# Layer 2's gathered rows as 1024 bytes of mirrored features, in fixed buffers

## The chip, the cores and the metric

The kernel runs on one core of a Trainium2 chip. The core has five engines that work side by side, each through its own instructions in program order: TensorE (PE, matrix products, with PEld for its weight loads), VectorE (DVE), ScalarE (ACT), GpSimd (POOL) and SyncE (SP). Sixteen DMA engines move data. An engine waits for another through semaphores. The metric is the device time of one execution in microseconds (us); the median of several runs counts.

## The reference

The reference is a graph attention network of two layers on 6250 nodes and 100,000 edges, sorted by destination. After a layernorm and relu of x, each layer computes, for node features h = x W:

```python
alpha_s = (h * a_src[None]).sum(-1)
alpha_d = (h * a_dst[None]).sum(-1)
e = jax.nn.leaky_relu(alpha_s[src] + alpha_d[dst], NEG_SLOPE)
m = jax.ops.segment_max(e, dst, num_segments=n)
e = jnp.exp(e - m[dst])
denom = jax.ops.segment_sum(e, dst, num_segments=n)
alpha = e / (denom[dst] + 1e-16)
out = jax.ops.segment_sum(h[src] * alpha[:, :, None], dst, num_segments=n)
```

Every node has an edge to itself beside the listed ones. Layer 1 has four heads of 64 features, layer 2 one head of 256. After layer 2 come relu, a product with Wm1 (256 x 256), bias, relu, a product with Wm2 (256 x 768), bias, and x is added. All is float32.

## The kernel before, in words

**Tiles.** The nodes make 49 node tiles of 128. The edges make 784 edge tiles of 128, of which 782 hold edges; two make a pair, four a group, eight a unit. On average a node tile takes 8 pairs. The numbers of pairs are used below as places: "pair 8t+28" is the 28th pair after the first pair of node tile t.

**Stages.** Stage 0 (to about 170 us) does the layernorm and the features of layer 1 (L447) and writes them as rows to a table in DRAM; a copy of them, `kept`, stays in SBUF. Layer 1's edges take from about 170 to 1390 us, layer 2's from there to the end.

**The two powers of a score.** The exponential of a leaky relu is max(exp(s), exp(0.2 s)), for s the sum of the source's and the destination's score. So a source needs e1 = exp(s) and e2 = exp(0.2 s), and an edge's weight is, up to a factor of its destination, w = max(e1, e2 * rho), where rho comes from the destination. Layer 1's end (Node1.steps, L948 to L973) computes for each node tile the features h of layer 2 and its score on PE, copies the features to `kept` on ACT (L969), makes e1 and e2 there with two exponentials (`powers`, L208 and L209), sets a one between them (DVE) and writes rows of 256 + 3 floats (features, e1, 1, e2: 1036 bytes) to layer 2's table.

**Gathers.** POOL fetches the rows of an edge tile's 128 sources with one indirect DMA (L645, in `gather`) into one half of a pair's buffer. The buffers are 20 of the pool "gathered", each [128, 2, 268] floats, used in turn by both layers; a gather is issued 8 groups ahead of its use, so that of pair q has to wait until PE is done with pair q - 20.

**A pair of layer 2** (`pair`): DVE makes v = e2 * rho (L712) and w = max(v, e1) (L715) for both edge tiles, then for each tile a matrix hw (L719) that holds w at the destination's column and zero elsewhere. PE multiplies it with the gathered rows into o_ps (L736), 258 columns: 256 features, e1, which nothing reads, and the one, which gives the sum of the weights. A product in float32 stands in the trace as two records, so a pair has four. A unit, four pairs, has one PSUM buffer.

**Sums and the node steps.** After each unit DVE adds its product to what is carried over (`take_sum`, acc, L753) and ACT copies quarters of 32 rows to the node's sum (L762). When a node's sum is whole, Node2.steps runs in six pieces, at the pairs that `STEPS_AT` (L62) lists: for node tile t at 8t + 20, 21, 24, 27, 30 and 33.

1. all_ adds the node's own edge (DVE, L1054) and rden is the reciprocal of the weights' sum (L1066).
2. o = all_ * rden (ACT, L1069), turned by PE (L915).
3. rT, relu and bias (ACT, L921), and the product with Wm1 (PE, L1078).
4. mT, relu and bias (ACT, L1083), the bias of y (PE, L1027) and the first half of the product with Wm2 (PE, L1088).
5. x is added to this half (DVE, L1092), and PE makes the other half.
6. x is added to that, and the result goes out (L1117).

Once per node tile PE also makes the destinations' terms of the next 16 edge tiles from two masks (`meet`, L691); SP brings two masks of 256 KB, x's 384 KB, and takes the result away.

**Order.** The schedule is manual: each engine runs its instructions in the order in which the program issues them. So pair 8t+28 on DVE stands behind the acc at 8t+27 and ahead of all_ of the next node tile, and on ACT mT and two sum copies stand at 8t+27.

**Layer 1's early rows.** Some pairs of layer 1 (`SOON`) are gathered early from a table that is not whole yet; 23 such buffers are put away to DRAM (`soon_away`) and fetched back (`soon_back`), and what they lack is added by PE and DVE (`soon_missing`, `soon_whole`). Layer 2's first tiles are treated likewise (`first_rows`, L389). A function `general` computes everything anew for graphs that don't fit; it is not executed here.

Of the kernel before, what the change touches and what calls it, by code (L numbers as in the profile page):

```python
# [70 lines left out]
def kernel(  # L71
# [12 lines left out]
    W2T: bass.AP,  # L84
    A2: bass.AP,
    b2: bass.AP,
    Wm1: bass.AP,
# [64 lines left out]

    RW = {1: 4 * (HID // 4 + 1), 2: HID + 2}
    TW = {1: RW[1] + 8, 2: RW[2] + 1}
    table, sd = {}, {}
# [55 lines left out]
    def heads_row(row):  # L211
        return row[:, :RW[1]].rearrange("p (h c) -> p h c", h=4)

    def edge_places(ones):

        dst_i = ones.tile([P, NET], I32, name="dst_i")
        dri = ones.tile([NCH, CH], I32, name="dri")
        nc.sync.dma_start(src_i, src_cols)
        yield
        yield  # L220
        soonest = sorted(range(len(SOON)), key=SOON.__getitem__)
        for i in range(0, len(SOON), 2):
            for k in soonest[i:i + 2]:
                soon_places(k)
            yield
        for to, of in ((dst_i, dst_cols), (dri, dst_rows)):
            nc.sync.dma_start(to, of)
            yield
            yield
        for layer in bT:  # L230
            with nc.allow_non_contiguous_dma(reason="256 numbers"):
                nc.sync.dma_start(bT[layer], {1: b1, 2: b2}[layer].rearrange("(k p) -> p k", p=P))
            yield
        b = ones.tile([P, OUT_DIM // P], F32, name="b")
# [12 lines left out]
        nc.sync.dma_start(dmod_d, drm)  # L247
        bp = ones.tile([P, 3, OUT_DIM // P], BF16, name="bp")
# [46 lines left out]
    def first_whole(pool, layer):  # L295

        j = 0
        for stage, (n, there) in enumerate(EARLY[layer]):
            for k in range(n):
                pair, t = divmod(FIRST + j, 2)  # L300
                G = first_G[layer][pair][:, t]
# [17 lines left out]
    def rows_in(layer):  # L319

        return gp.tile([P, 2, max(TW.values())], F32, name="G")[:, :, :TW[layer]]

    def first_rows(layer, stage):
# [3 lines left out]
        for j in range(j, j + n):  # L327
            k, t = divmod(FIRST + j, 2)
            if k not in first_G[layer]:
                first_G[layer][k] = rows_in(layer)  # L330
            nc.gpsimd.indirect_dma_start(
                out=first_G[layer][k][:, t], out_offset=None, in_=table[layer][:there * P],
                in_offset=bass.IndirectOffsetOnAxis(ap=first_i[layer][:, j:j + 1], axis=0))
# [3 lines left out]
    soon_d = dram.tile([len(SOON), P, 2 * TW[1]], F32, name="soon_d")  # L337
    soon_G, soon_of, soon_p, soon_hit = {}, {}, {}, {}
# [18 lines left out]
    def soon_away(held):  # L357

        for i in list(soon_G)[:max(len(soon_G) - held, 0)]:
            nc.sync.dma_start(soon_d[i], soon_G.pop(i).rearrange("p t c -> p (t c)"))  # L360

    def soon_back(i):
        G = rows_in(1)
        nc.sync.dma_start(G.rearrange("p t c -> p (t c)"), soon_d[i])
        return G

# [252 lines left out]
    def layer_edges(layer, H, node, pre, matched, pre_pool):  # L619
# [4 lines left out]
        with tc.tile_pool(name=f"eg{layer}", bufs=5) as eg, \  # L624
# [9 lines left out]
            def gather(g):  # L634
                if not 0 <= g < NG:
                    return
                for t in tiles(g):
# [5 lines left out]
                    if soon or k < FIRST + len(THERE.get(layer, ())):  # L643
                        continue
                    nc.gpsimd.indirect_dma_start(  # L645
                        out=G[k // 2][:, k % 2], out_offset=None, in_=table[layer],
                        in_offset=bass.IndirectOffsetOnAxis(ap=src_i[:, k:k + 1], axis=0))
# [277 lines left out]
    with tc.tile_pool(name="w2p", bufs=1) as wp, tc.tile_pool(name="wk2", bufs=2) as wk:  # L925
# [4 lines left out]
        class Node1:  # L930
# [17 lines left out]
            def steps(self, t, sum_, most=None, last=None):  # L948
# [18 lines left out]
                yield from rest(4)  # L967
                row = kept[t][:, :TW[2]]
                nc.scalar.activation(row[:, :HID], h_ps[:, :HID], AF.Copy)  # L969
                powers(row[:, HID:HID + 1], row[:, HID + 2:], h_ps[:, HID:HID + 1])  # L970
                nc.vector.memset(row[:, HID + 1:HID + 2], 1.0)
                nc.sync.dma_start(table[2][t * P:(t + 1) * P], row)
                nc.scalar.activation(sd[2][:, t], h_ps[:, HID:], AF.Copy)  # L973

        with tc.tile_pool(name="pre1", bufs=1) as pre:
            pre1 = prepare(pre, 1, 4)
            layer_edges(1, 4, Node1(), pre1,
                        lambda: scores_in(ps, w2, *w2_in, KH, 1), pre)


    with tc.tile_pool(name="wmp", bufs=1) as wp, tc.tile_pool(name="x3", bufs=4) as xp, \
# [48 lines left out]
        class Node2:  # L1030
# [27 lines left out]
            def steps(self, t, sum_, most=None, last=None):  # L1058
# [6 lines left out]
                rden = wk.tile([P, 1], F32, name="rden")  # L1065
                nc.vector.reciprocal(rden, all_[:, HID + 1:])  # L1066
                yield 1
# [62 lines left out]
def general(ctx, tc, v):  # L1130
# [6 lines left out]
    NTP = NT + 1  # L1137
    RWG = 4 * (HID // 4 + 1)
    with ExitStack() as own:
        def pool(name, bufs, **kw):  # L1140
# [5 lines left out]
        ps = pool("gps", 2, space=bass.MemoryType.PSUM)  # L1146
        gdram = pool("gdram", 1, space=bass.MemoryType.DRAM)
        pidx = keepp.tile([P, 2], F32, name="gpidx")
        nc.gpsimd.iota(pidx, pattern=[[P, 2]], base=0, channel_multiplier=1,
# [52 lines left out]
        def chunk(layer, H, c, b):  # L1202
# [6 lines left out]
            nc.vector.tensor_copy(df, di)  # L1209
            TWl = v["TW"][layer]  # L1210
            G = wk.tile([P, TPC, TWl], F32, name="G", tag="G")
# [133 lines left out]
        for i in range(NT):  # L1345
            rT = turned(1, 4, i)
            h_ps = ps.tile([P, HID + 2], F32, name="h_ps", tag="mm")
            for k in range(KH):
                nc.tensor.matmul(h_ps, rT[:, k], w2[:, k], start=(k == 0), stop=(k == KH - 1))
            row = wk.tile([P, v["TW"][2]], F32, name="row2")  # L1350
            nc.scalar.activation(row[:, :HID + 1], h_ps[:, :HID + 1], AF.Copy)
# [84 lines left out]
```

## Time and profile before

| | |
|---|---|
| median of 3 runs | 2554.95 us (2551.26 to 2574.33) |
| profiled execution, its own time | 2563.6 us |
| its span, first to last instruction | 2561.7 us |
| mean granted TensorE clock | 0.792 of full speed |
| busy: PE / DVE / ACT / POOL | 1797.7 / 1389.5 / 411.6 / 1523.5 us |
| gathers (L645) | 1507 records, 950 ns each |
| layer 2's o_ps (L736, 258 columns) | 1564 records, 460 ns each |
| hw of layer 2 (L719) | 782, 406 ns each |

Busy time counts an engine's instructions without their waits, so an engine that is 60% busy may still be the one that is always late. A group's line gives how often an instruction ran, its busy time and mean, and then the idle time of its engine just before it with what ended that idle time. The stages have to be read apart, since each has its own limit; the trace can be asked for any stretch of the span. A few records of matrix products and gathers can be missing from it.

### The profile page before, as it was taken

To read this page: it belongs to the slowest core of one execution; us is meant where nothing else is said; L and a number is where in the kernel's file an instruction comes from. 1 tells how busy PE (TensorE), PEld (TensorE's weight loads), DVE (VectorE), ACT (ScalarE), POOL (GpSimd) and SP (SyncE) were. 2 spreads that over 40 slices of the span, in tenths; PEclk is the share of its full clock that TensorE was granted. 3 is DMA by queue.
4 is the path that set the end of the run, shared out by engine and by line. 5 is a ranking of instruction groups with operands and counts; after the bars stand their busy time and mean duration, and the time that the engine had idled before them with its cause. 6 is when DMAs were issued, how large, how long until landed. Compare 5 with 4: busy or idle time off the path is not lost.

```text
span 2561.7 us, 26528 instructions
## 1 busy us (share of the span) xinstructions
PE 1797.7 (70%) x7728; PEld 1286.3 (50%) x7729; DVE 1389.5 (54%) x4195; ACT 411.6 (16%) x1273; POOL 1523.5 (59%) x1666
## 2 busy tenths in 40 slices
PE   9952768678667668686767456777667767776677
PEld 7841546556445446455554244544444444544455
DVE  7742667567656567666656444444444434444444
ACT  6730011011111111111111011111111111111112
POOL 5257465566655565656553666666666666666661
PEclk9975788878778778877889677777877777877888
DMA  9986355455545555555543445554545455545552
GB/s 340 355 266 199 114 154 148 125 150 154 140 138 136 146 141 151 154 148 157 133 122 122 129 122 153 156 150 135 153 140 168 133 152 157 153 133 152 149 149 75
DMA packets 167328, 400.36 MB, mean 156 GB/s; under 512 B 36632, under 2 KB 54255, under 8 KB 167175
## 3 DMA queue, kind: packets, MB, share of 16 engines
q0 software_dynamic: 75072, 211.10, 30.7%
q1 hardware_dynamic: 90732, 185.99, 21.5%
q10 hardware_dynamic: 1370, 1.48, 0.2%
q8 instruction: 65, 1.06, 0.2%
q14 instruction: 89, 0.72, 0.1%
HBM read 333.87 MB, written 64.56 MB: 156 GB/s over the span
## 4 chain that ended last, share of the span: by engine, by line
PE 38%; issue 22%; DVE 18%; another core or an unknown queue 11%; POOL 6%; DMA 4%; ACT 1%; DVEq 0%; SPq 0%; POOLq 0%; ACTq 0%
PE o_ps L736 19%; PE missing L389 6%; PE y_ps L1088 5%; POOL G L645 4%; DMA G<-table,src_i 4%; PE h_ps L447 4%; DVE hot L673 3%; DVE hw L724 3%; DVE soon_hit L379 2%; DVE e_ps L722 2%; DVE e_ps L712 2%; DVE hw L719 2%; PE tp L1078 1%; DVE acc L753 1%
## 5 line engine op out<-in xcount | busy, mean ns | idle before, releaser
L645 POOL DMA_INDIRECT G<-table,src_i x1507 | 1431.4, 950 | 861.5 <-issue 381.4
L736 PE MATMUL o_ps<-G,hw 128*128 128x258 f32 x1564 | 518.0, 460 | 247.7 <-issue 183.2
L736 PE MATMUL o_ps<-hw,hot 128*128 128x260 f32 x1564 | 489.9, 448 | 232.8 <-issue 157.3
L736 PEld LDWEIGHTS o_ps<-G,hw 128*128 128x128 f32 x1564 | 349.8, 230 | 385.5 <-issue 271.6
L736 PEld LDWEIGHTS o_ps<-hw,hot 128*128 128x128 f32 x1564 | 326.9, 218 | 361.5 <-issue 217.1
L762 ACT ACTIVATE sum<-acc 32x260 f32<-32x260 f32 (+1 forms) x384 | 160.0, 417 | 1224.7 <-DVE acc L753 697.7
L389 PE MATMUL missing<-kept,soon_hit 128*128 128x268 f32 x1028 | 277.0, 422 | 61.3 <-issue 60.6
L719 DVE TENSOR_SCALAR hw<-iota_ps,dcol,w 128x128 f32<-128x128 f32 x782 | 284.9, 406 | 16.9 <-DVE w L715 2.3
L724 DVE TENSOR_TENSOR hw<-G,e_ps 128x520 f32<-128x520 f32 x391 | 271.9, 695 | 27.7 <-DVE e_ps L722 11.8
L389 PEld LDWEIGHTS missing<-kept,soon_hit 128*128 128x128 f32 x1028 | 210.9, 208 | 119.4 <-issue 80.4
L1092 DVE TENSOR_TENSOR y<-y_ps,xt 128x384 f32<-128x384 f32 (+1 forms) x98 | 54.5, 556 | 256.5 <-PE o_ps L736 70.6
L1088 PE MATMUL y_ps<-wm,mT 128*128 128x384 f32 x392 | 180.2, 589 | 18.4 <-issue 9.5
L447 PE MATMUL h_ps<-w,r 128*128 128x264 f32 (+1 forms) x588 | 142.8, 398 | 17.8 <-issue 15.3
L673 DVE TENSOR_TENSOR hot<-iota_ps,dcol 128x512 f32<-128x512 f32 x196 | 133.6, 682 | 33.5 <-remote 24.5
L396 DVE SCALAR_TENSOR_TENSOR G<-G,soon_ok,missing 128x268 f32<-128x268 f32 x46 | 22.6, 492 | 212.7 <-remote 127.9
L447 PEld LDWEIGHTS h_ps<-w,r 128*128 128x128 f32 x588 | 111.8, 197 | 41.4 <-issue 17.6
L712 DVE TENSOR_TENSOR e_ps<-G,e_ps 128x8 f32<-128x8 f32 (+1 forms) x782 | 125.2, 160 | 7.3 <-DVE hw L724 2.8
L1088 PEld LDWEIGHTS y_ps<-wm,mT 128*128 128x128 f32 x392 | 78.2, 222 | 89.6 <-issue 50.2
L691 PE MATMUL e_ps<-win,mask 128*128 128x12 bf16 (+1 forms) x1564 | 67.8, 167 | 72.4 <-issue 69.1
L1083 ACT ACTIVATE mT<-tp,bm1c 128x128 f32<-128x128 f32 x98 | 30.6, 363 | 531.6 <-PE o_ps L736 260.8
L699 DVE TENSOR_REDUCE e_ps<-e_ps 128x64 f32<-128x192 f32 (+2 forms) x98 | 27.7, 283 | 136.4 <-remote 124.5
L691 PEld LDWEIGHTS <-mask 128*128 128x128 bf16 x1564 | 60.6, 98 | 79.7 <-issue 68.6
(415 smaller groups left out, 1347.4 us busy)
## 6 DMA issues: line engine op xcount, KB each, us to landing
xt<-in_x SPq DMA_DIRECT2D x96, 384.0 KB
drow<-dmod_d SPq DMA_DIRECT2D x49, 512.0 KB
mask_d<-mask SPq DMA_DIRECT2D x97, 256.0 KB
mask<-mask_d SPq DMA_DIRECT2D x97, 256.0 KB
G<-table,src_i POOLq DMA_INDIRECT x1507
xTt<-in_xT SPq DMA_DIRECT2D x49, 384.0 KB
out<-y SPq DMA_DIRECT2D x48, 384.0 KB
table<-kept SPq DMA_DIRECT2D x49, 134.0 KB
```

What stands on the lines that cost most here:

```text
L389: nc.tensor.matmul(soon_p[k], hit[:, T - there], kept[T], start=(T == there), stop=(T == NT - 1))
L447: nc.tensor.matmul(h_ps[:, :n], r[:, k], w1[:, k, :n], start=(k == 0), stop=(k == KI - 1))
L645: nc.gpsimd.indirect_dma_start(out=G[k // 2][:, k % 2], out_offset=None, in_=table[layer], in_offset=bass.IndirectOffsetOnAxis(ap=src_i[:, ...
L673: nc.vector.tensor_tensor(hot[g][:, T[0]:T[0] + n], iota_ps.unsqueeze(1).to_broadcast([P, n, P]), dcol[:, k:k + n].unsqueeze(2).to_broadca ...
L691: nc.tensor.matmul(e_ps[t][:, at + k, :3 * H], m[:, k * P:(k + 1) * P], pre.win[:, 2 * u + 2], start=True, stop=True)
L712: nc.vector.tensor_mul(v, e2, rho)
L719: nc.vector.tensor_scalar(hw[:, t], iota_ps, dcol[:, k:k + 1], w[:, t], ALU.is_equal, ALU.mult)
L724: nc.vector.tensor_mul(hw, Gp[:, :, :RW[1]].rearrange("p t (h c) -> p t h c", h=H), w.unsqueeze(3).to_broadcast([P, 2, H, C + 1]))
L736: nc.tensor.matmul(o_ps[u], l, r[:, :RW[layer]], start=(g % 2 == 0 and k == 0), stop=(g % 2 == 1 and k == tiles(g)[-1]))
L762: nc.scalar.activation(done[t][r], acc[r], AF.Copy)
L1088: nc.tensor.matmul(y_ps, mT[:, j], wm2[:, j, s * half:(s + 1) * half], start=False, stop=(j == KH - 1))
L1092: nc.vector.tensor_add(y[:n, s], y_ps[:n], xt[:n, s * half:(s + 1) * half])
```

## The change

Layer 2's rows lose everything but 256 floats, 1024 bytes. W2's columns are multiplied by a mirror (a Householder reflection) that maps the vector a_src of layer 2 on the first axis; feature 0 of a mirrored row is then the source's score divided by the length of a_src, up to its sign. The mirror is undone on each node tile's sum, before o. In parts:

- `mirror_in` computes in stage 0 the mirror's vector, the same scaled by -2 over its squared length (`mirror_b`), and two factors per partition (`slopes`) with which feature 0 becomes s and 0.2 s. It is some 22 instructions on DVE and two on ACT, and one broadcast DMA for a_src.
- `mirrored(wk, of, to)` reflects 128 rows: a product with mirror_b, a sum over 256, and a scaled addition, three DVE instructions. It is run on the two halves of W2 at the start of layer 1, and on all_ in step 1 of each of the 49 node tiles in layer 2, after rden and ahead of o.
- In each of the 391 pairs of layer 2, ACT makes e1 and e2 of both edge tiles from feature 0 of the gathered rows, with two exponentials of [128, 2] that take their scale from `slopes`; v and w on DVE read these.
- The one that gives the weights' sum is no longer gathered: the 20 buffers are now fixed, [128, 2, 288] floats, taken in turn by a list; layer 2's rows begin at float 16 of each half, and float 272 is set to one by 20 memsets on POOL at the start. o_ps has 257 columns.
- Node1.steps no longer makes the powers (98 instructions of ACT); its store writes rows of 256 floats.
- The set-aside rows of layer 1 go to DRAM and back as [128, 2, 268] views of the wider buffers. `general` gets a table of its own.

```diff
-    RW = {1: 4 * (HID // 4 + 1), 2: HID + 2}
-    TW = {1: RW[1] + 8, 2: RW[2] + 1}
+    RW = {1: 4 * (HID // 4 + 1), 2: HID + 1}
+    TW = {1: RW[1] + 8, 2: HID}
...
+    def mirror_in(ones, a):
...
+        nc.vector.tensor_mul(sq, a, a)
+        nc.vector.tensor_reduce(n2, sq, AX.X, ALU.add)
+        nc.vector.tensor_scalar(n2, n2, 1e-30, None, ALU.add)
+        yield
+        nc.scalar.activation(t, n2, AF.Ln)
+        nc.scalar.activation(r, t, AF.Exp, scale=-0.5)
+        yield
+        for _ in range(2):
...
+        nc.vector.tensor_scalar(mirror, a, r, None, ALU.mult)
+        nc.vector.tensor_scalar(sign, a[:, 0:1], 0.0, 2.0, ALU.is_ge, ALU.mult)
+        nc.vector.tensor_scalar(sign, sign, -1.0, None, ALU.add)
+        nc.vector.tensor_add(mirror[:, 0:1], mirror[:, 0:1], sign)
+        yield
+        nc.vector.tensor_mul(sq, mirror, mirror)
+        nc.vector.tensor_reduce(t, sq, AX.X, ALU.add)
+        nc.vector.reciprocal(scale, t)
+        nc.vector.tensor_scalar(mirror_b, mirror, scale, -2.0, ALU.mult, ALU.mult)
+        yield
+        nc.vector.tensor_mul(t, n2, r)
+        nc.vector.tensor_mul(t, t, sign)
+        for k, by in enumerate((-1.0, -SLOPE)):
+            nc.vector.tensor_scalar(slopes[:, k], t, by, None, ALU.mult)
+        yield
+
+    def mirrored(wk, of, to):
+
+        x = wk.tile([P, HID], F32, name="mirror_x")
+        nc.vector.tensor_mul(x, of, mirror_b)
+        along = wk.tile([P, 1], F32, name="along")
+        nc.vector.tensor_reduce(along, x, AX.X, ALU.add)
+        nc.vector.scalar_tensor_tensor(to, mirror, along, of, ALU.mult, ALU.add)
...
-    gp = edges_stack.enter_context(tc.tile_pool(name="gathered", bufs=2 * (AHEAD + 2)))
+    gp = edges_stack.enter_context(tc.tile_pool(name="gathered", bufs=1))
+    AT = {1: 0, 2: 16}
+    buffers = [gp.tile([P, 2, 288], F32, name=f"G{i}") for i in range(2 * (AHEAD + 2))]
+    for G in buffers:
+        nc.gpsimd.memset(G[:, :, AT[2] + HID:AT[2] + RW[2]], 1.0)
...
-        return gp.tile([P, 2, max(TW.values())], F32, name="G")[:, :, :TW[layer]]
+        buffers.append(buffers.pop(0))
+        return buffers[-1][:, :, AT[layer]:AT[layer] + max(TW[layer], RW[layer])]
...
-            nc.sync.dma_start(soon_d[i], soon_G.pop(i).rearrange("p t c -> p (t c)"))
+            nc.sync.dma_start(soon_d[i], soon_G.pop(i))
...
-                        out=G[k // 2][:, k % 2], out_offset=None, in_=table[layer],
+                        out=G[k // 2][:, k % 2, :TW[layer]], out_offset=None, in_=table[layer],
...
-                e1, e2 = ((Gp[:, :, RW[1]:RW[1] + 4], Gp[:, :, RW[1] + 4:]) if layer == 1 else
-                          (Gp[:, :, HID:HID + 1], Gp[:, :, HID + 2:]))
+                if layer == 1:
+                    e1, e2 = Gp[:, :, RW[1]:RW[1] + 4], Gp[:, :, RW[1] + 4:]
+                else:
+                    e = sm.tile([P, 2, 2, 1], F32, name="e")
+                    for k in range(2):
+                        nc.scalar.activation(e[:, k], Gp[:, :, 0:1], AF.Exp, scale=slopes[:, k])
+                    e1, e2 = e[:, 0], e[:, 1]
...
-                row = kept[t][:, :TW[2]]
-                nc.scalar.activation(row[:, :HID], h_ps[:, :HID], AF.Copy)
-                powers(row[:, HID:HID + 1], row[:, HID + 2:], h_ps[:, HID:HID + 1])
-                nc.vector.memset(row[:, HID + 1:HID + 2], 1.0)
+                row = kept[t][:, :HID]
+                nc.scalar.activation(row, h_ps[:, :HID], AF.Copy)
+                nc.vector.memset(kept[t][:, HID:RW[2]], 1.0)
...
+            def weights2():
+                scores_in(ps, w2, *w2_in, KH, 1)
+                for k in range(KH):
+                    mirrored(wk, w2[:, k, :HID], w2[:, k, :HID])
...
-                nc.vector.reciprocal(rden, all_[:, HID + 1:])
+                nc.vector.reciprocal(rden, all_[:, HID:])
+                mirrored(wk, all_[:, :HID], all_[:, :HID])
                 yield 1
```

More of the change, by code (lines that the diff above doesn't have):

```diff
@@ L85 @@
     A2: bass.AP,
+    a2: bass.AP,
     b2: bass.AP,
@@ L212, in heads_row, with col @@
         return row[:, :RW[1]].rearrange("p (h c) -> p h c", h=4)
+    def mirror_in(ones, a):
+        def col(name):
+            return ones.tile([P, 1], F32, name=name)
+        n2, r, t, sign, scale = (col(f"mirror_{k}") for k in ("n2", "r", "t", "sign", "scale"))
+        sq = ones.tile([P, HID], F32, name="mirror_sq")
+        nc.vector.tensor_mul(sq, a, a)
[6 more added lines that the diff above has]
+        for _ in range(2):
+            nc.vector.tensor_mul(t, r, r)
+            nc.vector.tensor_mul(t, t, n2)
+            nc.vector.tensor_scalar(t, t, -0.5, 1.5, ALU.mult, ALU.add)
+            nc.vector.tensor_mul(r, r, t)
+            yield
[13 more added lines that the diff above has]
+            nc.vector.tensor_scalar(slopes[:, k], t, by, None, ALU.mult)
+        yield
+    def mirrored(wk, of, to):
[4 more added lines that the diff above has]
+        nc.vector.scalar_tensor_tensor(to, mirror, along, of, ALU.mult, ALU.add)
     def edge_places(ones):
@@ L233, in edge_places @@
             yield
+        a2b = ones.tile([P, HID], F32, name="a2b")
+        nc.sync.dma_start(a2b, bcast(a2, HID))
+        yield
         b = ones.tile([P, OUT_DIM // P], F32, name="b")
@@ L247, in edge_places @@
         nc.sync.dma_start(dmod_d, drm)
+        yield
+        yield from mirror_in(ones, a2b)
         bp = ones.tile([P, 3, OUT_DIM // P], BF16, name="bp")
@@ L257 @@
     bT = {layer: const.tile([P, KH], F32, name=f"bT{layer}") for layer in (1, 2)}
-    gp = edges_stack.enter_context(tc.tile_pool(name="gathered", bufs=2 * (AHEAD + 2)))
+    gp = edges_stack.enter_context(tc.tile_pool(name="gathered", bufs=1))
[3 more added lines that the diff above has]
+        nc.gpsimd.memset(G[:, :, AT[2] + HID:AT[2] + RW[2]], 1.0)
+    mirror = const.tile([P, HID], F32, name="mirror")
+    mirror_b = const.tile([P, HID], F32, name="mirror_b")
+    slopes = const.tile([P, 2, 1], F32, name="slopes")
     rowsp = edges_stack.enter_context(tc.tile_pool(name="rows", bufs=3))
@@ L300, in first_whole @@
                 pair, t = divmod(FIRST + j, 2)
-                G = first_G[layer][pair][:, t]
+                G = first_G[layer][pair][:, t, :TW[layer]]
                 p = ps.tile([P, TW[layer]], F32, name="missing", tag="o", bufs=3)
@@ L331, in first_rows @@
             nc.gpsimd.indirect_dma_start(
-                out=first_G[layer][k][:, t], out_offset=None, in_=table[layer][:there * P],
+                out=first_G[layer][k][:, t, :TW[layer]], out_offset=None, in_=table[layer][:there * P],
                 in_offset=bass.IndirectOffsetOnAxis(ap=first_i[layer][:, j:j + 1], axis=0))
@@ L336 @@
     soon_ok = const.tile([P, len(SOON), 2], F32, name="soon_ok")
-    soon_d = dram.tile([len(SOON), P, 2 * TW[1]], F32, name="soon_d")
+    soon_d = dram.tile([len(SOON), P, 2, TW[1]], F32, name="soon_d")
     soon_G, soon_of, soon_p, soon_hit = {}, {}, {}, {}
@@ L359, in soon_away @@
         for i in list(soon_G)[:max(len(soon_G) - held, 0)]:
-            nc.sync.dma_start(soon_d[i], soon_G.pop(i).rearrange("p t c -> p (t c)"))
+            nc.sync.dma_start(soon_d[i], soon_G.pop(i))
     def soon_back(i):
         G = rows_in(1)
-        nc.sync.dma_start(G.rearrange("p t c -> p (t c)"), soon_d[i])
+        nc.sync.dma_start(G, soon_d[i])
         return G
@@ L976 @@
             pre1 = prepare(pre, 1, 4)
-            layer_edges(1, 4, Node1(), pre1,
-                        lambda: scores_in(ps, w2, *w2_in, KH, 1), pre)
+            def weights2():
+                scores_in(ps, w2, *w2_in, KH, 1)
+                for k in range(KH):
+                    mirrored(wk, w2[:, k, :HID], w2[:, k, :HID])
+            layer_edges(1, 4, Node1(), pre1, weights2, pre)
     with tc.tile_pool(name="wmp", bufs=1) as wp, tc.tile_pool(name="x3", bufs=4) as xp, \
@@ L1138, in general @@
     RWG = 4 * (HID // 4 + 1)
+    TWG = {1: v["TW"][1], 2: HID + 3}
     with ExitStack() as own:
@@ L1147, in general @@
         gdram = pool("gdram", 1, space=bass.MemoryType.DRAM)
+        table = {1: table[1], 2: gdram.tile([NT * P, TWG[2]], F32, name="gtable2")}
         pidx = keepp.tile([P, 2], F32, name="gpidx")
@@ L1209, in chunk @@
             nc.vector.tensor_copy(df, di)
-            TWl = v["TW"][layer]
+            TWl = TWG[layer]
             G = wk.tile([P, TPC, TWl], F32, name="G", tag="G")
@@ L1349, in general @@
                 nc.tensor.matmul(h_ps, rT[:, k], w2[:, k], start=(k == 0), stop=(k == KH - 1))
-            row = wk.tile([P, v["TW"][2]], F32, name="row2")
+            row = wk.tile([P, TWG[2]], F32, name="row2")
             nc.scalar.activation(row[:, :HID + 1], h_ps[:, :HID + 1], AF.Copy)
@@ L1421 @@
         "W2": f["W2"], "W2T": np.ascontiguousarray(f["W2"].T),
-        "A2": by_head(f["a_src2"], f["a_dst2"]), "b2": f["b2"],
+        "A2": by_head(f["a_src2"], f["a_dst2"]),
+        "a2": np.concatenate([f["a_src2"], f["a_dst2"]]).reshape(1, 2 * HID), "b2": f["b2"],
         "Wm1": f["Wm1"], "bm1": f["bm1"], "Wm2": f["Wm2"], "bm2": f["bm2"],
```

## The prediction

> **What bounds the kernel now.** I began with the page's busy shares and chain of waits.
>
> ```profile
> PE 1797.7 (70%) x7728; PEld 1286.3 (50%) x7729; DVE 1389.5 (54%) x4195; ACT 411.6 (16%) x1273; POOL 1523.5 (59%) x1666
> PE 38%; issue 22%; DVE 18%; another core or an unknown queue 11%; POOL 6%; DMA 4%; ACT 1%; DVEq 0%; SPq 0%; POOLq 0%; ACTq 0%
> ```
>
> No engine is full. PE and "issue" (time in which an engine waited for nothing recorded) lead the chain; DMA has 4%, ACT 1%. These are averages, so next I cut the span by stage: busy time of PE, PEld, DVE, ACT and POOL (with counts), granted clock, DMA share, GB/s.
>
> ```profile
> 50.00:110.00 60.00, 59.29 (x276) 49.42 (x275) 51.27 (x135) 45.41 (x157) 6.41 (x7) 1.00 0.99 341
> 200.00:1380.00 1180.00, 827.25 (x3617) 611.74 (x3618) 735.24 (x1919) 131.84 (x477) 684.73 (x722) 0.80 0.50 141
> 1450.00:2500.00 1050.00, 726.80 (x3048) 490.15 (x3047) 468.49 (x1766) 152.29 (x401) 688.04 (x726) 0.77 0.50 147
> 2512.00:2561.00 49.00, 39.17 (x168) 25.78 (x166) 24.63 (x84) 9.44 (x26) 0.00 (x0) 0.91 0.14 48
> ```
>
> The third row is layer 2, where the change acts on every pair: DVE is 45% busy, ACT 15%, DMA 50%. Then the groups of POOL and DVE in that stretch (busy us, mean ns, then idle before and its releasers):
>
> ```profile
> L645 POOL DMA_INDIRECT G<-table,src_i x726 | 689.1, 949 | 362.3 <-issue 181.4 <-remote 74.0 <-PE o_ps L736 53.2
> L712 DVE TENSOR_TENSOR e_ps<-G,e_ps 128x2 f32<-128x2 f32 x360 | 56.3, 156 | 0.1
> L1092 DVE TENSOR_TENSOR y<-y_ps,xt 128x384 f32<-128x384 f32 x88 | 48.9, 556 | 245.1 <-PE o_ps L736 70.6 <-remote 56.4 <-PE y_ps L1088 38.1
> ```
>
> A gather is issued every 0.95 + 0.30 = 1.25 us when nothing stops it (timeline): 726 x 1.25 = 907.5 us. The stretch lasts 1050, so POOL stood still for 142.5 us, for want of a buffer that PE had finished with. The first reader of a gathered row, L712, idled 0.1 us in 360 times: no gather landed last. So **the consumers set the pace of layer 2**. 16 gathers per node tile would take 20.0 us, and a node tile takes about 22.7. PE's own waits in the stretch say the same (total us, times, longest):
>
> ```profile
> PE o_ps L736 <- issue: 182.1, 168, 6.7
> PE o_ps L736 <- DMA G<-table,src_i: 11.0, 10, 1.7
> PE o_ps L736 <- DVE hw L719: 9.6, 7, 1.9
> ```
>
> The 182.1 us are stretches of 10 to 15 us after many of the mask products (L691), in which o_ps records come 0.7 to 2 us apart instead of 0.216 with all inputs there. What causes them no row shows.
>
> **The change, part by part: the gather.** A row shrinks from 1036 to 1024 bytes. 1072-byte rows of layer 1 took POOL 950 ns per gather and 1036-byte rows 949: nothing is saved on POOL. On the DMA engines, the gather queue moved 85.74 MB in 32.3% of 300 to 1300 us (16.6 bytes/ns per engine; rows of 1072, a multiple of 16) and 96.14 MB in 34.1% of 1450 to 2500 us (16.8; rows of 1036, a multiple of 4). By these rows 1.2% fewer bytes are 1.2% less engine time, and the landing is not waited for: 0 on the path.
>
> [...]
>
> **Two Exps per pair on ACT**, 128x2 with a per-partition scale. Exp of 128x1 (L209) took 143 ns; an activation with a per-partition operand (L420) 278. That bounds a pair at 0.29 to 0.56 us; I take 0.56, the row with such an operand: 782 x 0.28 = 219 us, which takes ACT in layer 2 from 15% to some 33%. That hides beside PE. The order does not hide: ACT works in program order, and the Exps of pair 8t+28 stand behind mT (L1083) and two sum copies (L762), so DVE, which now waits for ACT where it waited for a gather long landed, can no longer run ahead through them. DVE's queue behind that wait holds v, w, two hw, then all_; PE waits for hw and, through o, for all_.
>
> **Three DVE instructions per node tile** after rden: a 256-wide product (L939's and L945's 260-wide ones took 0.42 us), a sum of 256 (between 279 ns for 128 elements, L470, and 971 ns for 784, L1006: 0.41), a scaled sum (L1054, 0.48): 1.3 us x 49 = 64 us of a DVE that has 581 idle in the stretch. Hidden by amount, but not where they stand: ahead of pair 29.
>
> I worked this through on two node tiles. Here is the slower, from its timeline (start, duration, instruction, idle before):
>
> ```profile
> 1740.31 0.62 ACT L1083 ACTIVATE mT<-tp,bm1c 128x128 f32<-128x128 f32 x2 [18.98 <-remote]
> 1740.73 2.92 PE L1088 MATMUL y_ps<-wm,mT 128*128 128x384 f32 x4 [2.28 <-ACT mT L1083]
> 1740.96 0.86 ACT L762 ACTIVATE sum<-acc 32x258 f32<-32x258 f32 x2
> 1741.41 0.49 DVE L1054 SCALAR_TENSOR_TENSOR all__11925<-kept,own,sum 128x258 f32<-128x258 f32 x1 [15.45 <-ACT sum L762]
> 1741.93 0.16 DVE L1066 RECIPROCAL rden<-all__11925 128x1 f32<-128x1 f32 x1
> 1742.02 0.16 DVE L712 TENSOR_TENSOR e_ps<-G,e_ps 128x2 f32<-128x2 f32 x1
> 1743.45 3.35 PE L736 MATMUL o_ps<-G,hw 128*128 128x258 f32 x8
> ```
>
> Before: DVE had finished pair 28 and stood 15.45 us at all_; pair 29 began at 1742.02. PE took pair 28 (four records) at 1743.45 and pair 29 at about 1745.1. After: the sums end at 1741.82, the Exps of pair 28 at 1742.38; its v, w and hw (1.1 us) end at 1743.5, just in time; all_ and rden 0.6, to 1744.1; the mirror 1.3, to 1745.4; the first hw of pair 29 0.8 later, 1746.2. PE stands 1.1 us. In the quick tile at 1708 to 1718 the same steps run: sums end 1712.46, Exps 1713.0, pair 28 1714.1, all_ 1714.7, mirror 1716.0, first hw 1716.8, where PE came at 1715.75: again 1.1. Pair 29 begins 3.0 to 3.4 us later on DVE; PE had about 2 of them in hand. So the price per node tile lies between 0 (a later wait shrinks by as much) and 3.0 (PE loses its lead as well); I take 1.1, what both tiles give, x 47 = **52 us**.
>
> **The rest.** o_ps has 257 columns for 258: 1564 records x 0.216 us / 258 = -1.3 us. The mirror of W2 is two halves of 1.3 us on DVE at the start of layer 1, ahead of the first pairs: +2.6. The last two node tiles have their mirrors in the tail, where nothing follows: +2.6. mirror_in is some 22 small DVE instructions and two on ACT in the stage in which PE is 99% and DVE 85% busy: some 4 us beside PE, 0 taken, 4 if that cover fails. The 20 memsets meet a POOL busy 6.41 of 60 us: 0. One broadcast on SP in the first stage: 0 to 1. Node1 loses 98 ACT instructions of 143 ns, at places where ACT is 11% busy: 0. The set-aside rows of layer 1 go out and back as two runs of 1072 bytes per partition instead of one of 2144: 46 transfers issued long ahead, 0. POOL's gathers wait for one more engine, ACT, whose Exp on that buffer ended 20 pairs before: 0.
>
> Sum: 52 + 2.6 + 2.6 - 1.3 = +56 on the profiled execution's 2563.6 = 2619.6. That execution was 8.65 above the median of the three runs (2554.95), so in the median's terms **2611**.
>
> **Rivals.**
>
> *Hidden.* PE's lead covers the 1.1 us, or the unexplained stretches shrink by as much. [...] Against: both tiles above. Time: 2555 + 4 = 2559.
>
> *The gathers' traffic is what slows PE* (the other side). For: the slow stretches occur only while gathers run; in the tail, without them, the clock is 0.91, a node tile takes about 13 us, and none is seen. A packet of four 1036-byte rows has median 161 ns and mean 242: if aligned rows brought the mean to the median, a third of the gathers' engine time would go. If half of POOL's standing goes (some 150 us over the layer, so -75) and half of the 52 with it, the sum is -75 + 26 + 4 = -45: **2510**. With all of it gone, POOL's 1.25 us would pace the layer: 2409. It decides from the point at which more than a third of the 150 us goes, since that outweighs 52. Against: at 50 to 110 us DMA was 99% busy and PE ran at full clock without such stretches; 1072-byte rows, also badly placed, have median 166 and mean 254, so a row's place has shown nothing yet.
>
> *The lead is lost.* PE runs behind DVE from pair 29 to the next mask product: 3.0 x 47 = 141, + 4: 2700. For: DVE needs about 1.05 us for a pair and PE 0.86 at full clock, so a lost lead is not regained quickly. Against: at half clock PE needs 1.7.
>
> *It doesn't do what it says*: the gather costs as much as before on POOL and DMA. That is my forecast's own assumption, at the same 2611; it only excludes the second rival.
>
> **How the numbers follow.** Forecast 0.50 (2585 to 2650), hidden 0.18, faster by traffic 0.19, lead lost 0.13. The three runs spread over 0.9%, so about 1% is what can be told from no change; 2529 and 2581 are the bounds. Faster 0.21 (the traffic case and a corner of hidden), same 0.16, slower 0.63. The range must reach into the traffic case and towards the lost lead: 2505 to 2670 leaves out about half of the one and most of the other, 0.19.
>
> **What the profile after would show.** If right: ACT near 33% in layer 2; the first DVE instruction of a pair idles for ACT's Exp; three new DVE groups of together 1.3 us; PE's o_ps waits for DVE hw grow from 9.6 to some 50 us; the gather stays at 0.95 us and POOL's standing grows. The gather queue's share of the engines falls by about 1%, or by far more if a row's place matters. I would be wrong if the 182.1 us of unexplained issue time moved by tens of us either way: it is the largest loss in the stretch and nothing here says what it hangs on.

## The result, and the profile after

The changed kernel takes 2582.36 us (median of 20 runs, 2571.43 to 2594.51), the kernel before 2556.61 us (20 runs, 2543.02 to 2577.87): a ratio of 1.0092 with a 95% interval of 1.0069 to 1.0115. Forecast were 2611, faster 0.21, same 0.16, slower 0.63. The direction was right and the time lies in the range, but the loss is 24 us by this ratio (25.8 by the medians) where 56 were forecast.

The page of the changed kernel, busy shares and chain:

```profile
PE 1776.9 (69%) x7728; PEld 1278.1 (49%) x7729; DVE 1459.3 (56%) x4371; ACT 555.6 (22%) x1959; POOL 1528.6 (59%) x1686
DVE 30%; issue 23%; PE 21%; another core or an unknown queue 16%; ACT 4%; DMA 3%; POOL 3%; POOLq 0%; ACTq 0%; DVEq 0%; SPq 0%
```

Layer 2 of the changed kernel by the same columns as before (PE, PEld, DVE, ACT, POOL, granted clock, DMA share, GB/s), then the groups of POOL, DVE and ACT in this stretch, then PE's waits:

```profile
1450.00:2500.00 1050.00, 702.51 (x2990) 476.25 (x2990) 514.51 (x1854) 285.19 (x1105) 679.34 (x713) 0.79 0.47 144
```

```profile
L703 POOL DMA_INDIRECT G<-table,src_i x713 | 679.4, 953 | 370.8 <-issue 232.9 <-ACT mT L1151 63.8 <-remote 25.0
L775 DVE TENSOR_TENSOR e_ps<-e,e_ps 128x2 f32<-128x2 f32 x351 | 55.9, 159 | 337.1 <-ACT e L771 247.0 <-issue 78.6 <-ACT rT L984 11.4
L256 DVE TENSOR_REDUCE along<-mirror_x 128x1 f32<-128x256 f32 x44 | 18.5, 420 | 1.5
L771 ACT ACTIVATE e<-G,slopes 128x2 f32<-128x2 f32 x705 | 149.8, 284 | 0.6
```

```profile
PE e_ps L749 <- issue: 105.7, 85, 2.7
PE o_ps L799 <- issue: 89.5, 79, 2.4
PE o_ps L799 <- DVE hw L782: 47.1, 35, 5.6
```

The single parts have about the sizes that were forecast: an Exp takes 284 ns (0.28 was taken), the mirror's sum 420 ns (0.41). The Exps overlap, so that 705 of them keep ACT busy for 149.8 us, 0.43 us a pair where 0.56 was taken; ACT is 27% busy in the stretch (33% forecast). DVE's first instruction of a pair, which idled 0.1 us before, now idles 337.1, mostly for the Exps. PE waits 47.1 us for hw instead of 9.6, close to the 50 forecast.

The 182.1 us of "issue" at o_ps, of which the prediction said that it would be wrong if they moved by tens, are now 89.5. But the mask products (L691 before, L749 now) took over most of that, from this row of the kernel before to the 105.7 us above:

```profile
PE e_ps L691 <- issue: 26.7, 32, 1.9
```

Over all of PE's lines "issue" fell only from 247.8 to 235.9 us.

And yet the stretch lost little: 713 gathers went through it instead of 726. By the first and last all_, layer 2 lasts 1091.9 us (1469.0 to 2560.9) against 1072.4 (1466.9 to 2539.3): +19.5. The first all_ comes 2.1 us later (2.6 forecast), and from the last all_ to the end of the span both kernels take 22.4 us.

So the question for the runs was why a wait of PE that came nearly as forecast cost less than half of the forecast.

### The profile page after: what moved, and what is told of

It reads as the page before. It is cut to its first block, busy times and chain, and to the rows that moved or that the text cites. A ratio compares the mean times of both kernels' runs of the same rounds, so it can differ in the third digit from the quotient of the medians.

```text
span 2583.3 us, 27740 instructions
## 1 busy us (share of the span) xinstructions
PE 1776.9 (69%) x7728; PEld 1278.1 (49%) x7729; DVE 1459.3 (56%) x4371; ACT 555.6 (22%) x1959; POOL 1528.6 (59%) x1686
## 4 chain that ended last, share of the span: by engine, by line
DVE 30%; issue 23%; PE 21%; another core or an unknown queue 16%; ACT 4%; DMA 3%; POOL 3%; POOLq 0%; ACTq 0%; DVEq 0%; SPq 0%
PE o_ps L799 8%; DVE hw L782 6%; PE h_ps L505 5%; PE missing L447 4%; DVE hot L731 3%; DVE hw L787 3%; DMA G<-table,src_i 3%; POOL G L703 3%; DVE e_ps L775 2%; DVE soon_hit L437 2%; DVE e_ps L785 2%; DVE acc L816 2%; DVE w L778 2%; ACT e L771 2%
## 5 line engine op out<-in xcount | busy, mean ns | idle before, releaser
L799 PE MATMUL o_ps<-G,hw 128*128 128x257 f32 x1564 | 508.0, 462 | 184.0 <-issue 89.5
L775 DVE TENSOR_TENSOR e_ps<-e,e_ps 128x2 f32<-128x2 f32 x391 | 62.2, 159 | 363.1 <-ACT e L771 271.7
L1156 PE MATMUL y_ps<-wm,mT 128*128 128x384 f32 x392 | 172.9, 568 | 15.9 <-issue 8.7
L771 ACT ACTIVATE e<-G,slopes 128x2 f32<-128x2 f32 x782 | 167.1, 284 | 47.6 <-issue 37.3
L749 PE MATMUL e_ps<-win,mask 128*128 128x12 bf16 (+1 forms) x1564 | 75.2, 167 | 147.3 <-issue 144.5
L749 PEld LDWEIGHTS <-mask 128*128 128x128 bf16 x1564 | 66.1, 98 | 153.4 <-issue 144.2
```

The source lines that it names most:

```text
L749: nc.tensor.matmul(e_ps[t][:, at + k, :3 * H], m[:, k * P:(k + 1) * P], pre.win[:, 2 * u + 2], start=True, stop=True)
L771: nc.scalar.activation(e[:, k], Gp[:, :, 0:1], AF.Exp, scale=slopes[:, k])
L775: nc.vector.tensor_mul(v, e2, rho)
L799: nc.tensor.matmul(o_ps[u], l, r[:, :RW[layer]], start=(g % 2 == 0 and k == 0), stop=(g % 2 == 1 and k == tiles(g)[-1]))
L1156: nc.tensor.matmul(y_ps, mT[:, j], wm2[:, j, s * half:(s + 1) * half], start=False, stop=(j == KH - 1))
```

## The experiments

Several chips were used, and this matters: the kernel before takes 2557 to 2583 us on those that grant a mean clock of 0.80 and 2099 us on one that grants 0.88. The two kernels of a row always ran on one chip in one session; the chip of the rows with 2582.72 gave 2563.71 in a later session. Ratios are to the kernel before, with 95% intervals; the clock is that of the profiled execution.

| run | clock | median, us | before, us | ratio |
|---|---|---|---|---|
| mirror's three DVE instructions alone | 0.88 | 2108.87 | 2099.2 | 1.0051 (1.0036 to 1.0066) |
| Exps alone | 0.88 | 2101.29 | 2099.2 | 1.0017 (1.0006 to 1.0027) |
| rows and buffers alone | 0.88 | 2094.89 | 2099.2 | 0.9984 (0.9974 to 0.9995) |
| change, Exps three pairs earlier | 0.89 | 2109.91 | 2099.2 | 1.0059 (1.0044 to 1.0073) |
| change | 0.80 | 2600.65 | 2582.72 | 1.0063 (1.0041 to 1.0084) |
| nine DVE instructions instead of three | 0.80 | 2605.02 | 2582.72 | 1.0093 (1.0067 to 1.0118) |
| o_ps with fewer columns | 0.78 | 2573.77 | 2582.72 | 0.9982 (0.9958 to 1.0007) |
| rows and buffers alone | 0.79 | 2579.49 | 2582.72 | 0.9987 (0.9970 to 1.0003) |
| mirror's three instructions alone | 0.80 | 2564.34 | 2558.34 | 1.0010 (0.9985 to 1.0035) |
| half of o_ps's products | 0.77 | 2540.74 | 2558.34 | 0.9944 (0.9912 to 0.9976) |
| change, Exps three pairs earlier | 0.79 | 2574.79 | 2558.34 | 1.0060 (1.0032 to 1.0088) |
| no loads by SP in layer 2 | 0.80 | 2562.52 | 2563.26 | 0.9997 (0.9969 to 1.0025) |
| gathers of 512 bytes | 0.79 | 2561.22 | 2563.26 | 0.9992 (0.9971 to 1.0013) |
| change | 0.81 | 2582.93 | 2563.26 | 1.0095 (1.0067 to 1.0123) |
| 24 buffers instead of 20 | 0.80 | 2564.6 | 2563.71 | 1.0007 (0.9982 to 1.0032) |
| change, mirror's vector in PSUM | 0.80 | 2586.16 | 2563.71 | 1.0100 (1.0067 to 1.0134) |

**One part at a time.** To the kernel before, the mirror's instructions were added with vectors of zeros:

```diff
...
                 nc.vector.reciprocal(rden, all_[:, HID + 1:])
+                mirrored(wk, all_[:, :HID], all_[:, :HID])
                 yield 1
```

> The kernel before with the three DVE instructions after rden added in every node tile of layer 2 (the mirror's vectors are zeros, so the values stay as they were). Rows, buffers and powers as before. Theory 1 (lead and give-back): DVE is 1.3 us later per node tile, PE has about 2 us of hw in hand at this point, and what stall is left is partly given back because the clock is cut less; time +0 to +10 us. Theory 2 (the parts cost what was reckoned, and the shorter aligned rows gave some 27 us back): this part costs about half of 52, +20 to +35 us.

Then the Exps alone, from a row whose column 256 holds the score:

```diff
...
+                    for k in range(2):
+                        nc.scalar.activation(e[:, k], Gp[:, :, HID:HID + 1], AF.Exp, scale=slopes[:, k])
...
```

> The kernel before with the two Exps per pair on ACT alone: column 256 of a 1036-byte row holds the score, and ACT makes both powers from it with the same instruction as the change; no mirror, pool buffers as before. Theory 1: +0 to +15 us, DVE's first instruction of a pair idles for ACT by some 200 to 300 us in all, PE hardly waits. Theory 2: +20 to +35 us.

And the changed kernel without both:

```diff
-                        nc.scalar.activation(e[:, k], Gp[:, :, 0:1], AF.Exp, scale=slopes[:, k])
-                    e1, e2 = e[:, 0], e[:, 1]
+                    e1, e2 = Gp[:, :, HID:HID + 1], Gp[:, :, 0:1]
...
-                mirrored(wk, all_[:, :HID], all_[:, :HID])
```

> The changed kernel without mirror and without Exps: rows of 1024 bytes in fixed aligned buffers, v and w read columns of the buffer directly. It leaves out the powers of the scores and the reflections, so the weights are other numbers. Theory 1: rows and buffers are worth nothing on the path, -5 to +5 us against before. Theory 2: about -27 us.

These fell on the chip with 0.88: +9.7, +2.1 and -4.3 us by the medians. POOL there, in 1200 to 2000 us, for the mirror, the Exps and the rows in turn:

```profile
L658 POOL DMA_INDIRECT G<-table,src_i x636 | 608.0, 956 | 193.8 <-issue 145.0 <-PE o_ps L749 20.1 <-PE y_ps L1102 8.8
```

```profile
L649 POOL DMA_INDIRECT G<-table,src_i x640 | 606.2, 947 | 195.0 <-issue 115.2 <-PE o_ps L745 27.1 <-ACT e L717 21.3
```

```profile
L703 POOL DMA_INDIRECT G<-table,src_i x640 | 605.5, 946 | 194.9 <-issue 90.5 <-PE o_ps L796 68.8 <-PE y_ps L1150 8.8
```

640 gathers in 800 us are one every 1.25 us: POOL never stops (no idle time before a gather exceeds 0.6 us), and its gathers fill layer 2 (the last one ends within 1 us of the last all_). The mirror makes them 956 ns long instead of 946. 782 gathers x 10 ns = 7.8 of the 9.7 us: this is its price where POOL sets the pace. In the trace with the mirror alone, the gathers that overlap its last instruction (L225) take 1083 ns on average (such an overlap is called the collision below). In the trace of the changed kernel the same holds: gathers that overlap the last mirror instruction (L257) take 1028 ns on average, those that overlap none of the three 950.

**The order on ACT.** In the changed kernel the Exps are issued three pairs ahead:

```diff
...
+                    for k in range(q, min(q + 4, (LAST + 1) // 2)):
+                        powers_of(k)
...
-                    for k in range(2):
-                        nc.scalar.activation(e[:, k], Gp[:, :, 0:1], AF.Exp, scale=slopes[:, k])
+                    e = E.pop(q)
```

> The changed kernel with the Exps of a pair issued on ACT three pairs earlier, so that those of pair 8t+28 stand ahead of mT and of the sum copies. Everything else as in the change. If the order on ACT is what costs (Theory 1, the Exps' half of the lead), the time comes down to before +0 to +12 us, and DVE's idle time before v falls from 337 us in 1450 to 2500 to under 100. If the added work itself costs (mirror on DVE), it stays at +20 to +26 us.

> The changed kernel with the Exps issued three pairs earlier, +10.7 us at a clock of 0.88. At 0.80: if the lead lost through ACT's order costs on balance, it comes down to +0 to +10 us against the change's +16 to +26; if the clock gives that back anyway, it stays at +12 to +26.

+0.59% at 0.88 and +0.60% at 0.80. At 0.80 the change is +0.63% to +0.95%, and the intervals overlap: these runs don't tell a gain by the order on ACT from nothing. Yet at 0.80 the variant did what it was made for. In 1450 to 2500 us DVE's first instruction of a pair idles 0.1 us instead of 337.1, and PE's wait for hw is gone:

```profile
L786 DVE TENSOR_TENSOR e_ps<-e,e_ps 128x2 f32<-128x2 f32 x352 | 54.8, 156 | 0.1
```

```profile
PE o_ps L810 <- DVE hw L793: 4.3, 3, 2.0
```

So the wait that the forecast charged to the end can be taken away, and most of the loss stays. (At 0.88 the variant isn't as clean: there PE waits 157.2 us of 1200 to 2000 for rT, a wait that the kernel with the Exps alone doesn't have.)

**Less work and more.** The next runs ask what sets layer 2 at 0.80. Three times the mirror's instructions, 3.9 us of DVE per node tile:

> The kernel before with nine DVE instructions after rden in each node tile of layer 2 instead of the change's three (3.9 us instead of 1.3; values as they were). Theory 1, at a clock of 0.88: DVE waited 300 us for gathers in 1200 to 2000 us and takes most of the addition from that; +9.7 us grows to some +30. At a clock of 0.80: 1.9 us of stall per node tile beyond PE's lead, 89 us, of which the clock gives two thirds back: +30 us. If added time on DVE stood on the path fully, it would be +190 us.

It cost 22 us (+0.93%) for about 191 us (49 x 3.9) of DVE work. Next, PE alone was relieved, first of columns, then of products:

```diff
-                    nc.tensor.matmul(o_ps[u], l, r[:, :RW[layer]], start=(g % 2 == 0 and k == 0),
-                                     stop=(g % 2 == 1 and k == tiles(g)[-1]))
+                    first, last = g % 2 == 0 and k == 0, g % 2 == 1 and k == tiles(g)[-1]
+                    a = HID // 2 if layer == 2 and not first and not last else 0
+                    nc.tensor.matmul(o_ps[u][:, a:], l, r[:, a:RW[layer]], start=first, stop=last)
```

> The kernel before with less work for PE alone: in layer 2 six of a unit's eight products take 130 of the 258 columns (the first 128 features of those tiles are left out), every other instruction as before. If PE's clock sets layer 2 (granted 0.80), the cuts of the clock become rarer and layer 2 falls towards POOL's pace of 20.0 us per node tile: -80 to -130 us. If POOL's gathers set it (granted 0.88): 0 to -10 us. If the slow stretches have nothing to do with PE's own work, the clock rows stay as they are.

```diff
-                for t in range(2):
+                for t in range(2 if layer == 1 else 1):
...
```

> The kernel before with the product of every second edge tile of layer 2 left out on PE (values of those edges are missing); DVE, POOL and DMA do all they did. PE makes 782 fewer o_ps records and weight loads. If the clock's cuts answer to the number of PE's instructions and not to their columns (fewer columns had given nothing): layer 2 falls to POOL's pace, -60 to -120 us at a clock of 0.80. If the cuts have nothing to do with PE's own work: the half-clock time stays near 45% and the time within 1%. At 0.88: 0 to -10 us.

Fewer columns gave -0.18%, not told from nothing, and half the products -0.56%, though PE's busy time in 1450 to 2500 us fell from about 727 to 511.51 us. The granted clock fell in both to 0.72 in this stretch, which neither expectation had. The windows, PE's waits, two lines of PE's timeline and three of ACT's, all of the kernel with half the products ("remote" is a release that the profile can't put down to an instruction):

```profile
1450.00:2500.00 1050.00, 511.51 (x2367) 334.24 (x2367) 474.37 (x1788) 156.72 (x413) 689.88 (x727) 0.72 0.49 148
```

```profile
PE y_ps L1027 <- ACT mT L1083: 441.3, 39, 12.5
PE y_ps L1088 <- ACT mT L1083: 29.2, 4, 9.3
```

```profile
1721.78 1.55 PE L736 MATMUL o_ps<-G,hw 128*128 128x258 f32 x6
1734.72 0.47 PE L1027 MATMUL y_ps<-bm2r,ones_r 3*128 3x384 bf16 x1 [11.39 <-ACT mT L1083]
```

```profile
1688.07 0.63 ACT L1083 ACTIVATE mT<-tp,bm1c 128x128 f32<-128x128 f32 x2 [15.39 <-remote]
...
1711.01 0.63 ACT L1083 ACTIVATE mT<-tp,bm1c 128x128 f32<-128x128 f32 x2 [15.29 <-remote]
...
1734.04 0.63 ACT L1083 ACTIVATE mT<-tp,bm1c 128x128 f32<-128x128 f32 x2 [15.38 <-remote]
```

PE stands 441 of 1050 us for mT, and mT stands 15.3 us for the products of Wm1, whose records on PE are long past by then (1720.5 to 1721.5 for the mT at 1734.04). PE's semaphore updates, which tell the other engines that a product is done, stop at 1720.6 and come again at 1734.0 us, six within 0.3 us. In this kernel a stall of 1.1 us would have room in a stand of 10 us or more. In the kernel before the pauses are shorter (5.6 us at the median ahead of POOL's 22 long stops), so that the change's stall fell into such a pause is argued and not shown.

The clock does not explain the time here: this kernel has the lower clock (0.72 for 0.77) and is the faster one. In its trace the clock comes in windows of 3.4 us and is halved from 1728.1 to 1738.4, some 5 us after PE's last product (1723.3).

**What the stand hangs on.** Loads by SP taken away (masks and x of the first tiles stand in for all):

```diff
-        if u < NU:
+        if 5 <= u < NU:
+            mask[u] = standing[u % 4]
+        elif u < NU:
...
```

> The kernel before without SP's loads in layer 2: the masks of the first node tiles and the first tile of x stand in for all later ones (so the values are others); out still goes out. Theory 1 (the cuts of the clock begin with the burst of out, masks and x that SP issues once per node tile): the cuts become rare, layer 2 falls to POOL's pace, -60 to -120 us on a chip that grants 0.80. Theory 2 (they come from the load of the whole core over time, whatever SP does): within 1%.

Half the gathered bytes:

```diff
-                        out=G[k // 2][:, k % 2, :TW[layer]], out_offset=None, in_=table[layer],
+                        out=G[k // 2][:, k % 2, :(TW[1], HID // 2)[layer - 1]], out_offset=None,
+                        in_=table[layer] if layer == 1 else table[layer].rearrange("n (a c) -> (n a) c", a=2),
...
```

> Rows and buffers of the change without mirror and Exps (left out), and layer 2's gathers fetch 512 bytes per row instead of 1024 (the second half of each row stays what the buffer held). The rows alone were within 0.2% of before. If the gathers' traffic is what cuts PE's clock, layer 2 falls by 60 us or more on a chip that grants 0.80; if not, within 1% of before.

More buffers:

```diff
-AHEAD = 8
+AHEAD = 10
```

> The kernel before with gathers issued 10 groups ahead instead of 8, in 24 buffers instead of 20, in both layers. If POOL's stop comes from PE freeing buffers too late by a fixed time, four more buffers (5 us of gathers) cover it: -60 to -130 us at a granted clock of 0.80. If PE frees nothing until the gathers in flight have landed, the ring is only full later and the stop of about 3 us per node tile stays: within 1%. At 0.88 (no stops): within 0.5%.

None of the three moved the time by more than its interval. With 512 bytes a row the DMA share fell to 0.35:

```profile
1450.00:2500.00 1050.00, 726.36 (x3045) 488.83 (x3045) 467.14 (x1758) 153.93 (x405) 686.97 (x724) 0.76 0.35 102
```

What all kernels at 0.80 share is POOL: in 1450 to 2500 us every one issued 706 to 727 gathers, at about 1.25 us each when it ran, and stood some 136 to 168 us beyond that for want of buffers. In the kernel with half the products this is plainest: 39 of its 48 stops last 3.0 to 3.5 us, one for most node tiles. In the long stops (over 2.7 us) of the kernels without Exps, the next gather starts 1.5 to 1.9 us (medians) after the latest landing of a gather, and PE's updates come then, several at once: in the kernel before nine in the last microsecond (median). On the chip with 0.88 no pause of PE's updates in 1200 to 2000 us is longer than 6.4 us in the three kernels with single parts (8.0 with the Exps issued early). Why PE's updates come so late, and why one chip does not have this, stays open: PE's own work, SP's loads, bytes and buffers are excluded as its only cause.

**The change and before on one chip, and the collision.**

> The changed kernel once more, beside the runs that follow. The chip of the first four runs granted a clock of 0.88 instead of 0.80, and there POOL issued a gather every 1.25 us without a stop. Theory 1 (where the granted clock is near 0.88, POOL's gathers pace both layers, and the change costs only what stands on ends and starts): +8 to +13 us on such a chip, the sum of the three parts measured there (+9.7, +2.1, -4.3). On a chip that grants 0.80: +20 to +28 us, the recorded comparison again. Theory 2 (the recorded difference is one of executions): other values.

> The changed kernel, beside a trace of before from the same chip. At a granted clock near 0.80: +16 to +26 us; in layer 2 full-clock time up by 50 to 70 us and cut time down by 30 to 50 against b2_before. At 0.88: +5 to +13 us.

> The kernel before, unchanged, for its trace on this chip: at a clock near 0.80, some 45% of layer 2 in cut time; near 0.88, some 30%.

> The kernel before, unchanged, for a trace from the same chip as the three runs beside it. Theory 1 (the cut clock gives back): at a clock near 0.80, layer 2 has some 45% of its time at half clock and full-clock stretches of 3 or 4 windows of 3.4 us. At a clock near 0.88: about 30%, and POOL issues without a stop.

By the medians the change costs 17.9 us on the first of these chips, a little under the 20 to 28 expected, and 19.7 on the second. The windows and POOL, before and then the change, on the second:

```profile
1450.00:2500.00 1050.00, 730.93 (x3057) 491.48 (x3057) 468.65 (x1763) 154.39 (x407) 688.68 (x725) 0.76 0.50 148
...
L645 POOL DMA_INDIRECT G<-table,src_i x725 | 688.7, 950 | 362.8 <-issue 183.2 <-PE o_ps L736 69.4 <-remote 61.9
```

```profile
1450.00:2500.00 1050.00, 708.19 (x3026) 471.04 (x3025) 519.85 (x1876) 285.49 (x1111) 683.48 (x716) 0.80 0.47 144
...
L703 POOL DMA_INDIRECT G<-table,src_i x716 | 683.8, 955 | 370.2 <-issue 212.3 <-ACT mT L1151 46.2 <-ACT e L771 37.4
```

From first to last all_, layer 2 grows from 1070.8 to 1092.3 us. Where it grows is seen when the end of the last gather is taken as a mark (all from traces, us):

| kernel | start of the first all_ | from there to the last gather's end | from there to the end of the span |
|---|---|---|---|
| before, recorded pair | 1466.9 | 1043.6 | 51.2 |
| change, recorded pair | 1469.0 | 1055.6 | 58.7 |
| before, this chip | 1461.2 | 1042.5 | 48.8 |
| change, this chip | 1458.0 | 1055.6 | 60.1 |
| before, chip of the early Exps | 1449.7 | 1045.7 | 50.5 |
| change, Exps three pairs earlier | 1466.2 | 1059.8 | 52.7 |
| nine DVE instructions | 1469.0 | 1059.8 | 70.1 |

While POOL gathers, the change costs 12 to 13 us. In the last 700 gathers of the pair on this chip 3.5 us of that are longer gathers (5 ns each) and 11.5 are longer stops. Stops of over 3.5 us, of which before has none in the stretch, are 15 in the change. Behind the last gather the change costs another 7.5 to 11.3 us, in a stretch in which POOL issues nothing; with the Exps issued early it is 2.2, and with nine DVE instructions this stretch is some 20 us longer than in any kernel before here, almost their whole price.

The time at full clock in layer 2 grows from 575.9 to 659.0 us and that at half clock shrinks from 494.9 to 433.4, both by more than was expected. PE was busy for less of the stretch (708.19 for 730.93 us), so these traces don't show why the clock rose. That a higher clock gives time back was the author's estimate; no run shows it.

The collision was taken away with the mirror's vector in PSUM:

```diff
...
-        nc.vector.tensor_mul(x, of, mirror_b)
+        nc.vector.tensor_mul(x, of, mirror_ps)
...
-        nc.vector.scalar_tensor_tensor(to, mirror, along, of, ALU.mult, ALU.add)
+        nc.vector.scalar_tensor_tensor(to, mirror_ps, along, of, ALU.mult, ALU.subtract)
```

> The changed kernel with the mirror scaled so that one vector serves for both steps, and this vector in PSUM beside the column numbers, so that the product and the scaled addition read one operand from SBUF instead of two; the score's sign changes accordingly. If the collision of these instructions with the gathers is the mirror's price: gathers in layer 2 take 946 to 950 ns again instead of 955, 4 to 8 us less than the change (+16 to +26 us), so +8 to +20 us at a clock of 0.80; at 0.88 0 to +4 us instead of about +10. If the mirror costs by delaying hw, it stays at the change's time.

```profile
L709 POOL DMA_INDIRECT G<-table,src_i x715 | 677.0, 947 | 373.6 <-issue 241.5 <-ACT mT L1157 61.0 <-PE o_ps L805 20.4
```

Gathers are at 947 ns again (953 to 958 in the three traces of the change), so in these runs the collision goes with the second SBUF operand; the time is +1.00% (22 us, above the 8 to 20 expected), so where POOL stops anyway the collision is not the price.

**Two repeats.** Rows alone and the mirror alone at 0.80:

> Rows of 1024 bytes and fixed aligned buffers without mirror and Exps (those are left out), as in the first runs, for the case that this chip grants a lower clock. At 0.88 it was -4.3 us. At 0.80: -5 to +5 us by theory 1 (a gather's landing is not waited for); about -27 us if the rows gave back half of what mirror and Exps cost.

> The kernel before with the three DVE instructions after rden, values as they were; the first time at a clock of 0.88 it was +9.7 us. At 0.80 by theory 1: about a third to a half of the change's +16 to +26 us, since DVE is 64 us busier and the clock gives most of it back: +5 to +14 us; full-clock time in layer 2 up by 20 to 60 us, half-clock time down by most of that. If the parts add up to 52 without give-back: +25 us or more.

-0.13% and +0.10%, both within their intervals of nothing. Neither of these two parts alone makes the loss at 0.80. The Exps alone were not run there, so whether they make it or only all parts together is open. No complete kernel here beats the kernel before.

## Why the prediction was right and wrong

**What bounds.** "No gather landed last", read from L712's 0.1 us, was right, but the conclusion "the consumers set the pace of layer 2" was too short. PE is late, yet not because it has too much to do: with half its products POOL still stands 140 us in the stretch. The 20.0 us of POOL, which the prediction took for a floor beneath the real 22.7, are the larger part of every node tile; only the 2.7 above them is PE's, as a stop.

**The step that failed** is "the price per node tile ... I take 1.1, what both tiles give, x 47 = **52 us**". The way up to PE's wait for hw was sound: the wait rose by 37.5 us (9.6 to 47.1), 0.85 us for each of the 44 node tiles in the stretch. The step from this wait to the time was not. In its place the runs show +12.0 us up to the last gather, 0.26 us per node tile, and they show that the wait is not the price: with the Exps issued early it is 4.3 us, and the time stays at +0.60%. PE's total idle time in the stretch grew by 27 us, not by the sum of the new waits; for one thing, its waits for ACT shrank from 32.1 to 20.8 us. That a wait of PE counts only as far as it delays a buffer that POOL waits for fits all runs and was isolated by none. What else makes the 12 us, beside the longer gathers, stays open.

The rival "hidden" named such a thing ("the unexplained stretches shrink by as much"), and the measured loss lies between it and the forecast. But all of PE's "issue" time fell by 12 us in the recorded pair and rose by 12 (232.5 to 244.5) in the pair on one chip, so it isn't shown to be what took the stall in.

**The gather.** Nearly zero on the path was right: rows and buffers alone are 0.9984 and 0.9987. Bytes are not the limit: with 512-byte rows the DMA share fell from 0.50 to 0.35 and the time stayed. The rival by traffic, given 0.19, is excluded in that form. Per gather the queue's engine time fell by some 6% (34.1% of the stretch for 726 gathers before, 31.4% for 713 after), more than the 1.2% that the prediction took for 1.2% fewer bytes; nothing waits for it. A packet of four rows in 1450 to 2500 us took 159 ns at the median and 227 on average, 161 and 242 before. In layer 1 (300 to 1300 us), whose rows have 1072 bytes in both kernels, the average went from 254 to 267, so what a row's place is worth was not shown.

**The rest.** The tail was mis-sized: 2.6 us for two mirrors, where 7.5 and 11.3 us came behind the last gather. There the added work on ACT and DVE is hardly covered, and it holds more than the mirrors of two node tiles. That the first all_ came at +2.1 for 2.6 is luck: in the pair on one chip it came 3.2 us earlier, and over three executions of the kernel before it lies between 1449.7 and 1466.9. The cost of L254 to L257 for POOL was left out; at 0.88 it is most of the mirror's price.

## What to carry to other kernels

Before a stall is charged to the end, take work away from the engine that seems to bound, or take the stall itself away: if the time stays, that engine's waits are not the price list. An engine that issues transfers at a steady pace and stops only for want of buffers (here POOL, with a gather every 1.25 us and 136 to 168 us of stops in 1050) bounds the stage together with its stops, and a change is priced by what it does to these stops. The stretch behind the last transfer is priced apart (here 7.5 and 11.3 us of the loss). Judge a small change on more than one chip: here the same three instructions cost 9.7 us where POOL never stopped, most of it through longer gathers, and nothing that could be told from noise where it did stop.

## What was not expected of the hardware

The same kernel took 2099 us on one chip and 2557 to 2583 on others, and on the first POOL issued a gather every 1.25 us without a stop in the three kernels with single parts. On the others PE's semaphore updates came in bursts: in the kernel with half the products none is recorded from 1720.6 to 1734.0 us, then six within 0.3 us, 1.3 us after a gather's landing. Three DVE instructions, two of them with two SBUF operands, made gathers that overlapped them up to 14% longer (1083 for 946 ns on average with the last of them), and with one operand in PSUM the mean of all gathers in the stretch was 947 ns again.
